# Turning x1 between two layers by DMA transposes instead of on TensorE

## The chip, the cores and the metric

The kernel runs on one core of one Trainium2 chip. The metric is the device time of one execution in microseconds, as the median of several runs. The engines of the core work side by side, each through its own list of instructions in order: TensorE (PE: products and transposes, into PSUM), VectorE (DVE), ScalarE (ACT), GpSimd (POOL) and SyncE (SP), which here issues every DMA transfer. An engine that waits for a semaphore holds up everything behind it in its list. A DMA issued on SyncE goes to the core's 16 DMA engines; SyncE is free again after the issue, and the data lands later.

## The reference

Two graph attention layers over 128 graphs of 64 nodes with 768 features, float32 throughout, each followed by a residual and a layer norm:

```python
# layer 0, 12 heads of 64 features
h = einsum('bnd,ade->bane', x, W)
th = tanh(h)
attn = leaky(th @ w_src + swap(th @ w_dst))           # slope 0.2
attn = softmax(where(adj, attn, -999.0))
feat = elu(heads_joined(attn @ h + b))
gate = sigmoid(x @ H_w.T + H_b)
x = layernorm(x + gate * feat + (1 - gate) * x)       # x1 below

# layer 1, 6 heads of 128 features
q, k, v = x @ Wq + bq, x @ Wk + bk, x @ Wv + bv       # split in heads
probs = softmax(q @ k.T / sqrt(128) + where(adj, 0, -9e15))
x = layernorm(x + x + heads_joined(probs @ v) @ Wf + bf)
```

## The kernel before

The 8192 rows (graphs times nodes) are cut into 64 tiles of 128 rows, two graphs to a tile. Two tiles form a pair, and there are 32 pairs (`NP`).

Every large product is a `Job`: a 256 x 768 by 768 x 768 product (one pair by one weight), done in seven block products instead of eight, by sums of blocks. For that, sums of the input's blocks (`block_sums`, s1 to s4) and sums of the weight's blocks are made on VectorE or POOL. A block product is three matmuls into a PSUM bank; `step` issues one product and then the way out (evictions to SBUF by ScalarE and VectorE) of the product before it.

Layer 0 is a loop of turns, one per pair `p`. The order of TensorE is written out by hand, in lists such as `TURN`. A letter names the job, a digit the product: h (features of layer 0), g (gate), v (the values of layer 1), all in lower case for the jobs of this turn; u is the value job begun in the turn before, H and G are the feature job of the next pair and the gate job of the pair before. `plan` hangs other work onto a position of the list: after the product at that position, the functions of the plan issue their instructions on all engines. A turn does, for the new pair `p` (tiles n0, n1): features, gate, the attention logits (`products`, `terms`, `logits`, `leaky`, `masked`, `exps`); and for the old pair `q = p - 1` (tiles t0, t1): turning the probabilities (`probs_by_nodes`, on TensorE), `attend`, `features`, `elu1`, `gated`, `stats` and `normed`, which yields x1, and then:

- `by_features` (L814) turns x1 of a tile, 128 rows by 768 features, into x1T, features by rows, which the value products and layer 1 need as an operand. Six 128 x 128 transposes on TensorE (L738) go into two PSUM banks, and two ScalarE copies (L739) bring them to SBUF.
- `value_sums` (L855) and the steps `v_sums` make the four block sums of x1T on VectorE, in the tiles sv.
- five of the seven value products v stand in the same turn (`TURN` L77), the last two (u4, u3) at the start of the next turn.
- `spill_features` (L826), `spill_values` (L851) and the store in `normed` (L810) write x1T, v and x1 to DRAM for layer 1.

The logits need one half of their terms spread over all partitions: `terms` (L665) stores 128 x 12 sums to DRAM (dstd) and reads them back broadcast (dd, two DMAs). `with_bias` (L682) issues two DMAs a tile that swap halves of h into hx, which `attend` needs.

SyncE issues all of these in program order, and a DMA waits at issue for what it reads or overwrites. A buffer that is used again is waited for by its next writer: the tag `work` rotates five buffers of 128 x 768, `x1T` and the four sv tiles have one buffer each.

After the last pair, a turn without new pair (`LAST`) runs the first query and key products of layer 1; then layer 1 runs over 16 groups of four tiles.

Of the kernel before, what the change touches and what calls it, by code (L numbers as in the profile page):

```python
# [10 lines left out]
U8 = mybir.dt.uint8  # L11
AF = mybir.ActivationFunctionType
# [3 lines left out]
P = 128  # L16
# [50 lines left out]
    "u4", "u3", "q1", "q2", "k1", "k2", "q6", "q5", "q7", "Q1", "q4", "Q2", "q3", "k6", "k5", "k7",  # L67
    "Q6", "k4", "k3", "v1", "v2", "v6", "v5", "v7", "K1", "v4", "v3",
]
LAST_REST = [(1, 2), (0, 5), (1, 6), (0, 7), (1, 5), (1, 7), (0, 4), (0, 3), (1, 4), (1, 3)]  # L70
LAST_AT = {3: 3, 4: 4, 5: 6, 6: 8, 7: 9, 8: 11, 9: 12, 11: 15, 12: 16, 15: 20, 16: 20, 19: 22}
# [6 lines left out]
    "h1", "h2", "u4", "u3", "h6", "g1", "h5", "h7", "g2", "g6", "h4",  # L78
    "h3", "g5", "g7", "v1", "v2", "g4", "v6", "g3", "v5", "v7",
]  # L80

THIRD_AT = {pos: max(pos - 2, 0) for pos in range(len(TURN))}
TURNS = {
    0: (FIRST, FIRST_AT, {}),
    1: (SECOND, SECOND_AT, SECOND_OLD),
    2: (TURN[2:], THIRD_AT, THIRD_AT),
}


@with_exitstack  # L90
def kernel(
# [40 lines left out]
    x1T_d = [dram.tile([P, KC, PAIR * P], F32, name=f"x1Td_{p}") for p in range(NP)]  # L132
    v_d = [dram.tile([P, D], F32, name=f"vd_{t}") for t in range(2 * NP)]
# [40 lines left out]
    def all_of(steps):  # L174
        for s in steps:
            s()

# [350 lines left out]
    with ExitStack() as ph, ExitStack() as ph_r:  # L528
# [21 lines left out]
        def sums_of(eng, pool, tag, t, name):  # L550
            return block_sums(
                eng,
                sum_tiles(pool, tag, P, name),
                t[:, :HK, :P],
                t[:, HK:, :P],
                t[:, :HK, P:],
                t[:, HK:, P:],
            )
# [17 lines left out]
        A[0], x_steps = sums_of(G, sbr, "sx", xTs[0], "x0")  # L576
# [78 lines left out]

        def products(t):

            h = st[t]["h"]
            th = sbr.tile([P, 2, D], F32, tag="th", name=f"th_{t}")
            S.activation(th[:, 1, :].rearrange("p (a e) -> p a e", e=E0), h[:, :, :E0], AF.Tanh)  # L660
            V.tensor_tensor(th[:, 0, :], th[:, 1, :], wsd[:, 0, :], ALU.mult)  # L661
            G.tensor_tensor(th[:, 1, :], th[:, 1, :], wsd[:, 1, :], ALU.mult)  # L662
            st[t]["th"] = th

        def terms(t):  # L665

            th = st[t].pop("th")
            sd = small.tile([P, 2 * H0], F32, tag="sd", name=f"sd_{t}")
            V.tensor_reduce(sd, th.rearrange("p s (a e) -> p (s a) e", e=E0), AX.X, ALU.add)
            st[t]["sd"] = sd  # L670
            nc.sync.dma_start(out=dst_d[t], in_=sd[:, :H0])
            dd = work(f"dd_{t}")
            for g in range(2):
                nc.sync.dma_start(
                    out=dd[g * N : (g + 1) * N, :],
                    in_=dst_d[t][g * N : (g + 1) * N, :]
                    .rearrange("m a -> (m a)")
                    .partition_broadcast(N),
                )
            st[t]["dd"] = dd  # L680
# [131 lines left out]
        x1Ts, B = {}, {}  # L812

        def by_features(t):  # L814
# [4 lines left out]
            for half in range(2):  # L819
                transposed(  # L820
                    x1Ts[p][:, 3 * half : 3 * half + 3, i * P : (i + 1) * P],
                    x1[:, half * HALF : (half + 1) * HALF],
                    f"x1Tp_{t}_{half}",
                )

# [29 lines left out]
        def value_sums(q):  # L855
            B[q], v_sums[q] = sums_of(V, sb, "sv", x1Ts[q], f"v{q}")

        def x_sums(p):
            operands, steps = sums_of(G, sbr, "sx", xTs[p], f"x{p}")
            all_of(steps)  # L860
            A.setdefault(p, {}).update(operands)

        def third_begins():
            x = xTs[2]
            A[2] = {1: x[:, :HK, :P], 2: x[:, HK:, :P]}
            jobs["H"] = h_job(2)
# [13 lines left out]
        for p in range(NP + 1):  # L880
# [3 lines left out]
            if new:  # L884
                jobs["G"] = jobs.get("g")
                jobs["h"], jobs["g"] = jobs["H"] if p == 2 else h_job(p), gate_job(p)
            plan = {}

            turn, of_new, of_old = TURNS.get(p, (TURN, {}, {})) if new else (LAST, {}, LAST_AT)
# [5 lines left out]
            def was(pos, *acts):  # L895
                at(pos, old, *acts, places=of_old)

# [3 lines left out]
            def v_begins():  # L901
                value_sums(q)
                jobs["v"] = v_job(q)


            was(0, do(probs_by_nodes, t1))
            at(0, old, do(exps, t0), do(gate_tanh, t1), places={0: 6} if p == 1 else of_old)
            was(1, do(residual, t1))
            was(2, do(attend, t1), do(gate_tanh, t0))
            was(3, do(features, t1), do(probs_by_nodes, t0), do(residual, t0))  # L910
            was(4, do(elu1, t1), do(gated, t1))
            was(5, do(attend, t0), do(stats, t1))
            was(6, do(features, t0), do(normed, t1))
            was(7, do(elu1, t0), do(gated, t0))
            was(8, do(by_features, t1), do(stats, t0))
            was(9, do(normed, t0))
            was(12, do(v_begins))
            was(15, lambda: v_sums[q][0](), lambda: v_sums[q][1](), do(spill_features, q))
            was(16, lambda: v_sums[q][2]())
            was(19, lambda: v_sums[q][3]())  # L920

            at(0, p + 1 < NP, do(load_xT, p + 1))
            at(3, new, lambda: adjs.__setitem__(p, load_adj(sb, 2 * p, PAIR, f"adj_{p}")))
            at(6, new, do(mask, p))
            at(4, 0 <= p - 2 < NP, do(spill_values, p - 2))
            at(8, new, do(inputs, p))
            at(11, new, do(products, n1))
            was(11, do(by_features, t0))
            at(12, new, do(products, n0))
            at(13, new, do(terms, n1), do(with_bias, n1))  # L930
            at(14, new, do(terms, n0), do(with_bias, n0))
            at(15, new, do(plus_one, p))
            at(16, new, do(logits, n1))
            at(17, new, do(leaky, n1))
            at(17, p + 1 < NP, do(x_sums, p + 1), places={17: 12} if p == 0 else of_new)
            at(18, new, do(masked, n1), do(logits, n0))
            at(19, new, do(exps, n1), do(leaky, n0))
            at(20, new, do(masked, n0))

            if p == NP - 1:  # L940
# [3 lines left out]
                for pos, block in ((2, B11), (3, B21), (8, T3), (15, B22)):  # L944
                    at(pos, True, do(load_block, wq, w0_w, block))
                for pos, block in ((6, B11), (9, B21), (19, T3), (19, B22)):
                    at(pos, True, do(load_block, wk, hw_w, block))
                at(16, True, q_sums[0])
                at(18, True, queries_begin, q_sums[1])
                at(19, True, lambda: all_of(row_sums[:2]))  # L950
            if p == NP:
                flush()
                for act in plan.pop(0):
                    act()
# [8 lines left out]
            if p == 1:  # L963
                at(14, True, third_begins, places={})
# [122 lines left out]
```

## Time and profile before

| | |
|---|---|
| median of 3 runs | 2967.19 us (2966.39 to 2970.22) |
| the profiled execution | 2970.77 us |
| its span | 2969.0 us |
| layer 0, one turn (45.62 us): TensorE transposes of x1 | 12, busy 1.64 us |
| the same turn: ScalarE copies of x1T | 4, busy 1.72 us |
| DMA over the span | 284.81 MB, mean 96 GB/s |

How the page is read: the span is the time from the first to the last instruction of one profiled execution. An engine's busy time is the sum of the time in which it worked; matmuls are pipelined, so lengths of neighbouring matmuls overlap, and the distance from start to start tells what one costs. The chain of waits goes back from the last instruction, at each step to what released it. A row of a group reads: line, engine, operation, output and input tiles, shape, count, busy time, mean length of one, idle time before, and who ended that idle time. A row of DMA issues reads: output and input, queue, count, size of one, and the median time from issue to landing. The granted clock is 1.00 in layer 0's turns.

### The profile page before, as it was taken

To read this page: it belongs to the slowest core of one execution; us is meant where nothing else is said; L and a number is where in the kernel's file an instruction comes from. 1 tells how busy PE (TensorE), PEld (TensorE's weight loads), DVE (VectorE), ACT (ScalarE), POOL (GpSimd) and SP (SyncE) were. 2 spreads that over 40 slices of the span, in tenths; PEclk is the share of its full clock that TensorE was granted. 3 is DMA by queue.
4 is the path that set the end of the run, shared out by engine and by line. 5 is a ranking of instruction groups with operands and counts; after the bars stand their busy time and mean duration, and the time that the engine had idled before them with its cause. 6 is when DMAs were issued, how large, how long until landed. Compare 5 with 4: busy or idle time off the path is not lost.

```text
span 2969.0 us, 45314 instructions
## 1 busy us (share of the span) xinstructions
PE 2925.2 (99%) x18048; PEld 2023.0 (68%) x18048; DVE 1796.9 (61%) x3017; ACT 1009.0 (34%) x1761; POOL 811.1 (27%) x650
## 2 busy tenths in 40 slices
PE   7999999999999999999999999999999999999999
PEld 4566666666666666666578777787777887777875
DVE  6878888788788878887844344333343443443345
ACT  2344344444443444444422222222222222222221
POOL 2434333333343333333422212211111212121121
PEclk9999999999999999999999999999999999999999
DMA  5333333334333333343532211222212222112221
GB/s 171 122 109 114 107 121 115 103 118 128 104 119 104 121 113 106 115 129 103 176 97 77 70 60 55 86 86 76 68 52 64 86 76 73 59 57 82 87 80 48
DMA packets 179681, 284.81 MB, mean 96 GB/s; under 512 B 46736, under 2 KB 113296, under 8 KB 179472
## 3 DMA queue, kind: packets, MB, share of 16 engines
q1 hardware_dynamic: 179472, 281.93, 29.1%
q8 instruction: 143, 2.34, 0.3%
q14 instruction: 66, 0.54, 0.1%
HBM read 167.81 MB, written 101.06 MB: 91 GB/s over the span
## 4 chain that ended last, share of the span: by engine, by line
PE 94%; DVE 3%; DMA 1%; ACT 1%; issue 0%; SPq 0%; POOLq 0%; POOL 0%; DVEq 0%; ACTq 0%
PE y_k L222 8%; PE y_o L222 8%; PE y_q L222 8%; PE y_v L222 8%; PE y_h L222 8%; PE y_g L222 8%; PE z_v L222 4%; PE z_o L222 4%; PE z_k L222 4%; PE z_h L222 4%; PE z_q L222 4%; PE z_g L222 4%; PE x_k L222 2%; PE x_o L222 2%; PE x_q L222 2%; PE x_h L222 2%
## 5 line engine op out<-in xcount | busy, mean ns | idle before, releaser
L789 POOL TENSOR_TENSOR x<-gate,x 128x768 f32<-128x768 f32 x64 | 117.4, 1835 | 323.8 <-ACT gate L840 309.0
L457 POOL TENSOR_TENSOR y<-y,bf_bc 128x768 f32<-128x768 f32 x64 | 115.3, 1832 | 311.4 <-DMA y<-x1d 311.4
L481 DVE TENSOR_TENSOR y<-y_o,y 128x384 f32<-128x384 f32 x128 | 71.4, 557 | 202.1 <-PE y_o L222 198.0
L339 DVE TENSOR_TENSOR kT<-z_k,kT 128x256 f32<-128x256 f32 x96 | 40.8, 425 | 239.3 <-PE z_k L222 136.1
L662 POOL TENSOR_TENSOR th<-th,wsd 128x768 f32<-128x768 f32 x64 | 117.2, 1832 | 182.5 <-DVE th L661 182.5
L274 POOL TENSOR_TENSOR rs_b<-ve_b,minus_half 128x1 f32<-128x1 f32 x64 | 35.1, 548 | 452.5 <-DVE ve_b L272 451.7
L192 POOL TENSOR_TENSOR sq_q<-a,a 128x768 f32<-128x768 f32 x16 | 29.2, 1828 | 432.8 <-PE y_o L222 286.9
L222 PE MATMUL y_h<-w_wq,xT 128*128 128x384 f32 x384 | 136.3, 492 | 8.6 <-DMA w_wq<-in_w_dram 7.9
L222 PE MATMUL y_k<-a,hw_wk 128*128 128x256 f32 x576 | 144.6, 387 | 0.0
L222 PE MATMUL y_q<-a,w_wq 128*128 128x256 f32 x576 | 140.9, 381 | 1.9 <-ACT qT L338 1.9
L222 PE MATMUL z_v<-wv,sv_v 128*128 128x384 f32 x384 | 138.9, 498 | 3.2 <-DVE v L652 3.2
L222 PE MATMUL y_q<-sq_q,w_wq 128*128 128x256 f32 x576 | 140.3, 380 | 0.9 <-ACT qT L338 0.9
L222 PE MATMUL y_h<-w_wq,sx_x 128*128 128x384 f32 x384 | 136.5, 492 | 4.2 <-ACT h L622 4.2
L222 PE MATMUL z_q<-sq_q,w_wq 128*128 128x256 f32 x576 | 140.1, 379 | 0.0
L222 PE MATMUL y_k<-sq_q,hw_wk 128*128 128x256 f32 x576 | 140.1, 379 | 0.0
L222 PE MATMUL z_k<-sq_q,hw_wk 128*128 128x256 f32 x576 | 140.0, 379 | 0.0
L338 ACT ACTIVATE qT<-y_q,bq_c 128x256 f32<-128x256 f32 x144 | 67.4, 469 | 213.2 <-PE y_q L222 213.2
L222 PE MATMUL y_v<-wv,sv_v 128*128 128x384 f32 x384 | 136.6, 492 | 3.0 <-DVE sv_v L193 3.0
L386 ACT ACTIVATE sc<-sc 128x512 f32<-128x512 f32 x48 | 30.2, 630 | 319.3 <-DVE sc L385 319.3
L222 PE MATMUL z_h<-w_wq,sx_x 128*128 128x384 f32 x384 | 137.6, 495 | 0.9 <-DVE w_wq L168 0.9
L222 PE MATMUL y_g<-hw_wk,sx_x 128*128 128x384 f32 x384 | 134.9, 488 | 2.4 <-DVE hw_wk L171 2.2
L222 PE MATMUL y_v<-wv,x1T 128*128 128x384 f32 x384 | 136.1, 491 | 1.2 <-ACT x1T L739 1.0
(171 smaller groups left out, 6678.1 us busy)
## 6 DMA issues: line engine op xcount, KB each, us to landing
x<-in_x_dram SPq DMA_DIRECT2D x64, 384.0 KB, 3.6
dd<-dstd SPq DMA_DIRECT2D x128, 192.0 KB, 3.4
x1d<-x SPq DMA_DIRECT2D x64, 384.0 KB, 2.6
x1Td<-x1T SPq DMA_DIRECT2D x32, 768.0 KB, 4.8
vd<-v SPq DMA_DIRECT2D x64, 384.0 KB, 2.9
a<-x1Td SPq DMA_DIRECT2D x64, 384.0 KB, 3.6
v<-vd SPq DMA_DIRECT2D x384, 64.0 KB, 2.3
y<-x1d SPq DMA_DIRECT2D x64, 384.0 KB, 4.1
```

The source lines that it names most:

```text
L192: lambda: e.tensor_tensor(s1, a21, a22, ALU.add),
L222: T.matmul(to[:, : self.n], lhsT, rhs, start=kc == 0 and not more, stop=kc == HK - 1, skip_group_check=more,)
L274: G.tensor_tensor(rstd, ve, minus_half, ALU.pow)
L338: lambda mn, bk_: S.activation(at(*mn), bk_, AF.Identity, bias=bias(mn[1])),
L339: lambda mn, bk_: V.tensor_tensor(at(*mn), bk_, at(*mn), ALU.add),
L386: S.activation(sc, sc, AF.Exp, scale=SCALE)
L457: G.tensor_tensor(y, y, pools["bf"], ALU.add)
L481: V.tensor_tensor(at(*mn), b, at(*mn), ALU.add)
L662: G.tensor_tensor(th[:, 1, :], th[:, 1, :], wsd[:, 1, :], ALU.mult)
L789: G.tensor_tensor(xp, st[t]["gate"], xp, ALU.mult)
```

## The change

For 28 pairs, 2 to 29, x1 is no longer transposed on TensorE. Float32 x1 is taken as words of 16 bits, and the low and the high halves are copied apart (`apart`), stored to DRAM (`send`), read back turned by six transposing DMAs (`turned`), each of 512 rows (low halves of 256 rows, then high halves) by 128 features, and joined to float32 again by four ScalarE copies (`joined`). The turned halves land in the tile sv, which later takes the four block sums as before. Pairs 0, 1, 30 and 31 still use `by_features`.

All seven value products of a pair now stand in the turn after the one that makes its x1; the first two products of the next pair's features (H1, H2) close a turn. The plan of the first two turns is kept in `of_opening`; all later ones follow `of_turn`. `products`, `terms` and `x_sums` are split so that their parts can stand at different positions.

```diff
 TURN = [
-    "h1", "h2", "u4", "u3", "h6", "g1", "h5", "h7", "g2", "g6", "h4",
-    "h3", "g5", "g7", "v1", "v2", "g4", "v6", "g3", "v5", "v7",
+    "h6", "h5", "g1", "u1", "h7", "u2", "g2", "u6", "h4", "u5", "h3", "u7",
+    "g6", "g5", "g7", "u3", "u4", "H1", "H2", "g4", "g3",
 ]
...
+    halves_d = [dram.tile([2, PAIR * P, D], U16, name=f"halvesd_{p}") for p in range(NP)]
...
+    def words(t):
+        return t.bitcast(U16).rearrange("p (e two) -> p two e", two=2)
...
+        def apart(t):
+            sp = work(f"sp_{t}").bitcast(U16).rearrange("p (two e) -> p two e", two=2)
+            x1 = words(st[t].pop("x1"))
+            if t % 2:
+                G.tensor_copy(sp[:, 0], x1[:, 0])
+            else:
+                S.copy(sp[:, 0], x1[:, 0])
+            S.copy(sp[:, 1], x1[:, 1])
+            st[t]["halves"] = sp
+
+        def send(t):
+            p, i = divmod(t, 2)
+            nc.sync.dma_start(
+                out=halves_d[p][:, i * P : (i + 1) * P, :].rearrange("h t d -> t h d"),
+                in_=st[t].pop("halves"),
+            )
+
+        def turned(p, *chunks):
+            if p not in sv:
+                sv[p] = sb.tile([P, 4, HK, P], F32, tag="sv", name=f"sv_{p}", bufs=1)
+            for c in chunks:
+                nc.sync.dma_start_transpose(
+                    out=landing(p)[:, c],
+                    in_=halves_d[p][:, :, c * P : (c + 1) * P].rearrange("h t f -> (h t) f"),
+                )
+
+        def landing(p):
+            return (
+                sv[p].rearrange("p s k t -> p (s k t)").bitcast(U16).rearrange("p (c ht) -> p c ht", c=KC)
+            )
+
+        def joined(p):
+            x1Ts[p] = sb.tile([P, KC, PAIR * P], F32, tag="x1T", name=f"x1T_{p}", bufs=1)
+            dst = x1Ts[p].bitcast(U16).rearrange("p c (t two) -> p two c t", two=2)
+            land = landing(p).rearrange("p c (two t) -> p two c t", two=2)
+            for kh in range(2):
+                for half in range(2):
+                    rows = slice(kh * HK, (kh + 1) * HK)
+                    S.copy(dst[:, half, rows], land[:, half, rows])
...
+            by_pe = old and q in (0, 1, NP - 2, NP - 1)
+            by_dma = old and not by_pe
...
+            def of_turn():
+                at(0, True, do(exps, t0))
+                at(0, p + 1 < NP, do(load_xT, p + 1))
+                at(1, True, do(probs_by_nodes, t1))
+                at(2, True, do(gate_tanh, t1), do(residual, t1))
+                at(3, True, do(attend, t1))
+                at(4, True, do(features, t1), do(probs_by_nodes, t0))
+                at(4, new, lambda: adjs.__setitem__(p, load_adj(sb, 2 * p, PAIR, f"adj_{p}")))
+                at(5, True, do(elu1, t1), do(gated, t1), do(gate_tanh, t0), do(residual, t0))
+                at(6, True, do(attend, t0), do(stats, t1))
+                at(7, True, do(features, t0), do(normed, t1))
+                at(7, new, do(mask, p))
+                at(8, True, do(elu1, t0), do(gated, t0))
+                at(8, by_dma, do(apart, t1))
...
+                at(9, True, do(stats, t0))
+                at(9, by_dma, do(send, t1))
+                at(9, new, do(tanh, n1), do(products, n1), do(inputs, p))
+                at(10, True, do(normed, t0))
+                at(11, by_dma, do(apart, t0))
+                at(12, by_dma, do(send, t0))
+                at(12, new, do(tanh, n0))
...
+                at(13, new, do(terms, n1), do(products, n0))
+                at(14, new, do(spread, n1))
+                at(15, new, do(terms, n0))
+                at(15, p + 1 < NP, do(next_begins, p + 1), do(x_sums, p + 1, 0))
+                at(16, new, do(spread, n0))
+                at(16, by_dma, do(turned, q, *range(KC)))
+                at(16, new, do(with_bias, n1), do(with_bias, n0), do(plus_one, p), do(logits, n1))
...
+                at(17, new, do(leaky, n1))
...
+                at(18, new, do(masked, n1), do(logits, n0))
+                at(18, True, do(spill_values, p - 2))
+                at(19, new, do(exps, n1))
...
+                at(20, new, do(leaky, n0), do(masked, n0))
+                at(20, by_dma, do(joined, q), do(v_begins))
+                at(20, p + 1 < NP, do(x_sums, p + 1, 1))
+                at(21, by_dma, v_sum(0), v_sum(1), do(spill_features, q), places={21: len(turn)})
+                at(22, by_dma, v_sum(2), places={22: len(turn) + 1})
+                at(23, by_dma, v_sum(3), places={23: len(turn) + 2})
```

A place of `len(turn)` or more is position 0, 1 or 2 of the next turn. `THIRD`, `NO_NEXT` and `LAST` are the lists of the third turn, of the last pair's turn and of the turn without a new pair; they are rewritten to the same pattern, `LAST` with 31 products for 27.

## The prediction

> **What bounds the kernel now.** I read the page's busy table and chain of waits first, then the busy time of one stretch, TensorE's and SyncE's timelines inside it, and last the rows that price a transfer.
>
> ```profile
> span 2969.0 us, 45314 instructions
> ...
> PE 2925.2 (99%) x18048; PEld 2023.0 (68%) x18048; DVE 1796.9 (61%) x3017; ACT 1009.0 (34%) x1761; POOL 811.1 (27%) x650
> ...
> PE 94%; DVE 3%; DMA 1%; ACT 1%; issue 0%; SPq 0%; POOLq 0%; POOL 0%; DVEq 0%; ACTq 0%
> ```
>
> TensorE is busy nearly all of the span and is 94% of the chain that ended last. Whatever leaves it is won, and whatever makes it wait is lost. Next, busy time by stretch. The columns are length, then busy time of PE, PEld, DVE, ACT and POOL, then granted clock, DMA share and GB/s.
>
> ```profile
> 701.68:747.30 45.62, 45.62 (x247) 27.69 (x246) 36.91 (x54) 20.02 (x32) 16.54 (x14) 1.00 0.35 114
> ...
> 1440.00:1530.00 90.00, 80.66 (x383) 54.77 (x380) 63.59 (x86) 29.93 (x52) 35.97 (x19) 0.94 0.36 123
> ```
>
> The first row is one turn of layer 0 (attention of one tile to the same point a pair later). TensorE has no idle time in it; VectorE has 8.7 us to spare, ScalarE 25.6, POOL 29. The waits that exist lie in the first 160 us and around the end of layer 0, the second row. So in the turns there is no wait to remove, and a gain can only come from work taken off TensorE. That work, in TensorE's timeline (start, length, engine, line):
>
> ```profile
> 716.12 0.82 PE L738 MATMUL x1Tp<-ident,x 128*128 128x128 f32 x6
> 716.77 2.10 PE L222 MATMUL y_g<-hw_wk,sx_x 128*128 128x384 f32 x6
> 718.71 2.10 PE L222 MATMUL y_h<-w_wq,xT 128*128 128x384 f32 x6
> ...
> 722.58 0.82 PE L738 MATMUL x1Tp<-ident,x 128*128 128x128 f32 x6
> 723.24 2.10 PE L222 MATMUL z_g<-hw_wk,sx_x 128*128 128x384 f32 x6
> ```
>
> Starts count, since lengths overlap. Six transposes of a tile hold TensorE for 716.77 - 716.12 = 0.65 us, the second tile's 0.66. One product (a step of the turn) takes 718.71 - 716.77 = 1.94 us.
>
> **What is removed.** 28 of the 32 pairs (2 to 29) are turned by DMA, the other four as before. TensorE loses 28 x (0.65 + 0.66) = 36.7 us. No product is added or dropped: seven per job, only the values' seven all stand one turn later. ScalarE loses four evictions of 0.482 us a pair.
>
> **What is added, and what covers it.** Per pair: three ScalarE copies and one POOL copy that part x1 into halves, two stores, six transposing DMAs on SyncE, and four ScalarE copies that join the halves. A ScalarE pass over 128x768 takes 0.84 us (the group of L849), so ScalarE gains 7 x 0.84 - 1.93 = 3.95 us and is at 24 of 44; POOL gains 1.0 to 1.8 us (its passes over 128x384 and 128x768). Both stay well below TensorE, so their volume costs nothing. VectorE's work is unchanged, but the four sums of x1T, 1.31 + 1.24 + 0.88 + 0.54 = 4.0 us, move to the start of the next turn. Their first reader there is u6 in step 8, the join's first reader is u1 in step 4.
>
> What decides is one date: when the last transpose has landed. I lay out one new turn, t = 0 at its first product, 45.62 - 1.31 = 44.3 us long. Step k ends at 1.94 k plus what is put in: 0.66 and 0.8 for the transposes of the probabilities after steps 2 and 5, 0.86 for each attention after steps 4 and 7.
>
> - The turn's logits come first on SyncE. Gate product g7 (step 15) ends at 32.4. The second tile's chain has by then run through ScalarE's tanh (31.3, after x1's norm at 28.3, its two halves and an eviction), VectorE's product (32.4), POOL's product of 1.83 (34.2) and VectorE's sum of 1.74: it ends at 36.0. That sum is stored and read back:
>
> ```profile
> 731.57 0.54 SPq L671 DMA_DIRECT2D dstd<-sd  x1
> 734.03 1.10 SPq L674 DMA_DIRECT2D dd<-dstd  x2
> ...
> 736.50 0.54 SPq L827 DMA_DIRECT2D x1Td<-x1T  x1
> 737.13 0.39 SPq L539 DMA_DIRECT2D xT<-in_xT_dram  x1
> 737.57 1.01 SPq L282 DMA_DIRECT2D adj<-in_adj_dram  x1
> ```
>
> - SyncE issues in order. From store to end of the second read-back issue it takes here 735.13 - 731.57 = 3.6 us (2.6 in the other tile of this turn), so the first transpose goes out at about 39.2. The two stores of the halves (issued by 30) and u3, the last reader of the tile it lands in (step 16, 34.4), are past by then.
> - The join waits for the landing on ScalarE, behind the second tile's leaky logits, which end at about 45.2 whatever the transposes do. Behind the join stand the exponentials of that tile, the eviction of h6 and the two evictions of the first tile's probabilities: 3.4 + 0.84 + 0.47 + 0.95 = 5.7 us. TensorE needs the last at the first attention, at 44.3 + 8.4 = 52.7. So the landing may be as late as 47.0, that is 7.8 us after the first issue; from there each us late is one us of TensorE per turn. At 9.1 (7.8 + 1.31) the gain is used up.
> - Queued on SyncE behind the transposes: four hx reads (first needed at that attention), two stores of values, the store of x1T, which waits for the join, and behind it the next xT (6.9 us to land, needed some 25 us later) and adj. The value store is waited for by u1's eviction on ScalarE; it has about 5 us to spare. They become late only after the join does.
>
> No transposing DMA is in the trace. The nearest rows:
>
> ```profile
> x<-in_x_dram SPq DMA_DIRECT2D x64, 384.0 KB, 3.6
> ...
> x1Td<-x1T SPq DMA_DIRECT2D x32, 768.0 KB, 4.8
> ...
> v<-vd SPq DMA_DIRECT2D x384, 64.0 KB, 2.3
> ...
> xT<-in_xT_dram SPq DMA_DIRECT2D x31, 768.0 KB, 6.9
> ```
>
> Six times 128 KB are the 768 KB of x1Td and xT, so the low bound is 4.8 us. By issues: five at 0.55 and the last landing in 2.3 (64 KB) to 3.6 (384 KB) gives 5.0 to 6.4. If each issue costs SyncE 1.01 as adj does, 5 x 1.01 + 3.6 = 8.7. The high bounds are six that do not overlap: 6 x 2.3 = 13.8 or 6 x 3.6 = 21.6. I take 6.4, as six issues back to back are nearest to dd's pair, which does overlap. That leaves 1.4 us to spare.
>
> The Trainium skill has two rules here that disagree, and no run shows either yet. "VectorE: DVE Perf Modes", section The three transpose paths, puts a 128x128 two-byte transpose at 1309 ns by DMA against 390 ns on TensorE and advises TensorE; the 24 such blocks of a pair, one after another, would be an estimated 31 us and would cost over 600 us in all. "DMA: Bandwidth & Descriptors", section Latency and other measured facts, gives 261 GB/s for DMA transposes of rows that are not contiguous, which is what is read here; 786 KB would then be an estimated 3.0 us and hide with my 6.4.
>
> Outside the turns: the last stretch has 9.3 us idle TensorE now, and the list of its last turn is rewritten (31 steps for 27). I add one more wait of the size of its 2.4 us row, with 5 us either way.
>
> **The sum.** The profiled execution took 2970.8 us, its span 2969.0 and 1.8 around it; it is 3.6 above the median of 2967.2, which the runs are measured by. From the profiled time: 2970.8 - 36.7 + 2.4 = 2936.5; from the median, 2932.9. I predict 2933 us for the median.
>
> **Rivals.**
>
> A, the landing is a little late: issues at 1.01, 8.7 us, 0.9 us of wait a turn: 2967.2 + 28 x (0.9 - 1.31) + 2.4 = 2958; at 9.1, no change. For it: SyncE has rows of 1.01 and of 0.55, and the read-backs of dd share the DMA engines at that moment. Against it: those engines are 35% busy over the turn.
>
> B, slower: the transposes do not overlap, and the join on ScalarE takes over as the bound. Place: ScalarE's wait for the last landing, then TensorE before the first attention. It decides from 9.1 us. At 13.8 us the wait is 6.0 a turn: 2967.2 + 28 x (6.0 - 1.31) + 2.4 = 3101. Idle time also costs clock:
>
> ```profile
> 1486.00:1488.50 2.50, 0.10 (x1) 0.02 (x1) 2.43 (x4) 0.00 (x0) 2.50 (x2) 1.00 0.00 1
> 1490.10:1493.50 3.40, 3.40 (x11) 2.72 (x10) 3.40 (x3) 1.15 (x3) 3.32 (x2) 0.58 0.02 5
> ```
>
> After 2.4 us of idle TensorE, 3.4 us ran at a granted 0.58; counted as half, that is up to 28 x 1.7 = 48 us more, 3149. For B: this is an operation no row shows, with sources in rows of 256 bytes, and only 1.4 us of cover. Against it: ordinary transfers from this queue do overlap (dd's two reads go out 0.55 apart and land 3.6 after issue).
>
> C, hidden anyway: would TensorE have waited in the place of the transposes? Its turns have no idle time and the engines slack, so this gives 2967, and I give it only the part of "same".
>
> **How the numbers follow.** Forecast (landing within 7.8 us) 0.45; A 0.17, of which 0.10 is still faster by over 0.2% (below 2961) and 0.07 within 0.2% of before, about what a measurement of this kernel can tell from no change; C 0.01; B and late cases beyond 9.4 us 0.37. So faster 0.55, same 0.08, slower 0.37. The forecast's own range is 2925 (36.7 won, 5 less waiting at the ends) to 2940. The range goes to 3060: a landing at 11 us, 3.2 us of wait a turn and most of the clock's loss (2967 + 53 + 40); of B, about half lies above it.
>
> **What would show it.** Right: no x1Tp group but for the four pairs, no wait of ScalarE at the join beyond 2 us, turns of 44.3 us without idle TensorE, first issue to last landing under 7.8 us. Wrong: probabilities' evictions named as what TensorE waits for, ScalarE waiting for a DMA into sv, SyncE's issues of the transposes at 1 us or more each, a granted clock below 1.00 inside the turns. A first transpose issued well before or after 39.2 would move the limit with it.

## The result, and the profile after

The changed kernel takes 3079.38 us (median of 4, 3075.88 to 3086.19) against 2968.68 us of the kernel before beside it: 1.0376 times, 95% interval [1.0364, 1.0389]. It is slower by 111 us where 34 us less were forecast, and 19 us above the range. The profiled execution has this page (span, busy time, chain of waits):

```profile
span 3076.6 us, 45130 instructions
...
PE 2943.9 (96%) x17712; PEld 2016.0 (66%) x17712; DVE 1780.3 (58%) x3017; ACT 1124.8 (37%) x1845; POOL 884.0 (29%) x678
...
PE 70%; DVE 16%; ACT 5%; issue 4%; DMA 2%; POOL 1%; SPq 1%; DVEq 0%; POOLq 0%; ACTq 0%
```

TensorE has 336 instructions fewer, as meant, and yet is busy 19 us longer. Its share of the chain fell from 94% to 70%, and VectorE's rose from 3% to 16%. So TensorE both waits and runs more slowly. What it waits for in the turns (stretch 160 to 1440 us; total, times, longest):

```profile
PE y_g L239 <- DVE gate L655: 73.4, 26, 2.8
PE av L786 <- ACT pT L766: 0.5, 1, 0.5
```

This is one wait of 2.8 us in every turn, for VectorE's eviction of a gate product (26 turns lie in the stretch). The probabilities (pT), which the prediction watched, appear once, with 0.5 us. Three timelines of one turn show where that eviction was held up (start, length, engine, line). TensorE:

```profile
755.67 2.10 PE L239 MATMUL y_v<-wv,sv 128*128 128x384 f32 x6
757.61 2.10 PE L239 MATMUL y_g<-hw_wk,sx_x 128*128 128x384 f32 x6
759.54 2.10 PE L239 MATMUL z_g<-hw_wk,sx_x 128*128 128x384 f32 x6
764.47 3.90 PE L239 MATMUL y_g<-hw_wk,sx_x 128*128 128x384 f32 x6 [2.83 <-DVE gate L655]
```

ScalarE and then VectorE, of the same kernel:

```profile
760.36 1.03 ACT L295 ACTIVATE x<-x,sh_a,rs_a 128x768 f32<-128x768 f32 x1 [3.39 <-DVE sh_a L294]
761.42 0.83 ACT L860 COPY sp<-x 128x768 uint16<-128x768 uint16 x1
762.16 0.83 ACT L861 COPY sp<-x 128x768 uint16<-128x768 uint16 x1
762.89 0.47 ACT L668 COPY v<-y_v 128x384 f32<-128x384 f32 x1
```

```profile
763.39 0.56 DVE L669 TENSOR_TENSOR v<-z_v,v 128x384 f32<-128x384 f32 x1 [2.60 <-ACT v L668]
763.87 0.55 DVE L655 TENSOR_TENSOR gate<-y_g,hb_bc 128x384 f32<-128x384 f32 x1
764.33 1.74 DVE L689 TENSOR_REDUCE sd<-th 128x24 f32<-128x1536 f32 x1
```

Read it backwards. The second y_g is gate product g7. It needs the bank in which g6 (757.61) stands, so it waits for VectorE's addition of g6 (L655, 763.87). On VectorE that addition is queued behind the addition of the value product u7 (L669), which needs ScalarE's copy of u7 (L668). TensorE finished u7 at 757.77, but ScalarE ran that copy only at 762.89, because it stands in program order behind x1's norm of the pair's first tile (L295) and the two copies of its halves (L860, L861). ScalarE itself sat idle for 3.39 us waiting for that norm's input. So a product that was ready at 757.77 was evicted 5.1 us late by an idle engine, and two more engines queued behind it. In the kernel before, the norms ran at 713.49 and 719.30 of the turn shown there and its next eviction of values only at 729.24: no value product stood near a norm.

The same turn by busy time, then the wait and what follows it (length; busy PE, PEld, DVE, ACT, POOL; granted clock; DMA share; GB/s):

```profile
730.95:779.82 48.87, 46.04 (x236) 27.24 (x235) 35.46 (x54) 23.34 (x35) 18.88 (x15) 0.97 0.45 138
761.64:764.47 2.83, 0.00 (x0) 0.00 (x0) 1.07 (x3) 2.83 (x5) 0.21 (x1) 1.00 0.54 209
764.47:767.90 3.43, 3.43 (x6) 1.97 (x7) 2.47 (x2) 1.10 (x2) 0.88 (x1) 0.54 0.18 59
```

After the 2.83 us without work TensorE gets 0.54 of its clock for 3.43 us: g7 takes 768.21 - 764.47 = 3.74 us from start to start instead of 1.94, another 1.80 us. Between the first and the 26th of these turns (the halves' first copy, 175.77 and 1397.70) lie 25 turns, 48.88 us each in the mean, from 47.16 to 50.20. The wait is 2.8 us in all of them; what differs is the clock behind it, here after the waits that end at 185.35, 232.51 and 714.29:

```profile
185.35:188.80 3.45, 3.45 (x11) 2.12 (x12) 3.42 (x4) 1.10 (x2) 0.90 (x1) 1.00 0.18 59
232.51:235.90 3.39, 3.39 (x6) 1.96 (x7) 2.47 (x2) 1.10 (x2) 0.84 (x1) 0.53 0.18 60
714.29:719.50 5.21, 5.21 (x8) 2.86 (x9) 3.40 (x4) 1.10 (x2) 2.66 (x2) 0.50 0.25 86
```

So the 1.80 us of the turn shown is near the mean of a loss that runs from 0.1 to 3.1 us. Without wait and loss a turn comes to 48.87 - 2.83 - 1.80 = 44.24 us, and the turn from 185.35 to 232.51, which has hardly any loss, gives the same: 47.16 - 2.82 - 0.10. The forecast was 44.3. The turns lose 28 x (48.88 - 45.62) = 91 us. The rest, 16 us by the two profiled executions and 20 by the medians, lies outside them; it is what is left over, not a sum of waits. TensorE's wait for the gate in the third turn (3.8 us, none before) belongs to it, and these waits from 1440 to 1640 us:

```profile
PE y_q L239 <- DMA a<-x1Td: 12.2, 1, 12.2
PE y_g L239 <- DVE gate L655: 5.6, 2, 2.8
PE x1Tp L765 <- ACT x L295: 3.8, 1, 3.8
```

The two waits of y_g here are the last two of the 28 turns; the other two lie at the end of layer 0, where the longest wait in the kernel before was 3.2 us. Last, the transposes: SyncE's timeline, the issues' own figures (ns, least, median and most; then us to landing), and ScalarE's join that waits for them.

```profile
722.83 1.08 SPq L701 DMA_DIRECT2D dd<-dstd  x2
724.02 8.08 SPq L876 DMA_TRANSPOSE sv<-halvesd  x6
```

```profile
L876 SPq DMA_TRANSPOSE sv<-halvesd x168: 1144/1258/2433, 194.2 to 1522.6; - x168
...
DMA to landing us min/median/max: 2.6/2.8/4.6
```

```profile
730.23 1.98 ACT L893 COPY x1T<-sv 128x768 uint16<-128x768 uint16 x2 [0.19 <-DMA sv<-halvesd]
733.68 1.98 ACT L893 COPY x1T<-sv 128x768 uint16<-128x768 uint16 x2 [1.47 <-DMA sv<-halvesd]
```

The last one landed 733.68 - 724.02 = 9.66 us after the first went out. That is later than the 7.8 us that the prediction allowed, and yet TensorE does not wait for it here.

### The profile page after: what moved, and what is told of

It is laid out like the page before. It is cut to its first block, busy times and chain, and to the rows that moved or that the text cites. A ratio compares the mean times of both kernels' runs of the same rounds, so it can differ in the third digit from the quotient of the medians.

```text
span 3076.6 us, 45130 instructions
## 1 busy us (share of the span) xinstructions
PE 2943.9 (96%) x17712; PEld 2016.0 (66%) x17712; DVE 1780.3 (58%) x3017; ACT 1124.8 (37%) x1845; POOL 884.0 (29%) x678
## 4 chain that ended last, share of the span: by engine, by line
PE 70%; DVE 16%; ACT 5%; issue 4%; DMA 2%; POOL 1%; SPq 1%; DVEq 0%; POOLq 0%; ACTq 0%
PE y_o L239 8%; PE y_k L239 8%; PE y_q L239 8%; PE y_g L239 7%; PE y_v L239 4%; PE z_o L239 4%; PE y_h L239 4%; PE z_k L239 4%; PE z_q L239 4%; DVE ex L826 3%; PE z_v L239 2%; DVE fo L803 2%; PE x_o L239 2%; PE x_k L239 2%; DVE st_a L285 2%
## 5 line engine op out<-in xcount | busy, mean ns | idle before, releaser
L239 PE MATMUL y_g<-hw_wk,sx_x 128*128 128x384 f32 x384 | 178.4, 613 | 81.5 <-DVE gate L655 79.0
L816 POOL TENSOR_TENSOR x<-gate,x 128x768 f32<-128x768 f32 x64 | 136.6, 2135 | 373.8 <-ACT gate L909 373.8
L239 PEld LDWEIGHTS y_g<-hw_wk,sx_x 128*128 128x128 f32 x384 | 86.3, 233 | 157.4 <-DVE gate L655 96.3
L683 POOL TENSOR_TENSOR th<-th,wsd 128x768 f32<-128x768 f32 x64 | 116.8, 1824 | 181.6 <-DVE th L682 181.6
L810 ACT ACTIVATE ex<-fo,minus_one 128x768 f32<-128x768 f32 x64 | 59.9, 935 | 276.5 <-DVE fo L803 276.5
L239 PE MATMUL y_q<-a,w_wq 128*128 128x256 f32 x576 | 143.6, 387 | 12.2 <-DMA a<-x1Td 12.2
L239 PE MATMUL z_v<-wv,sv 128*128 128x384 f32 x384 | 144.6, 516 | 0.0
L712 POOL TENSOR_TENSOR h<-h,b_bc 128x768 f32<-128x768 f32 x64 | 140.3, 2214 | 0.0
```

Of the source, the lines that this page charges most:

```text
L239: T.matmul(to[:, : self.n], lhsT, rhs, start=kc == 0 and not more, stop=kc == HK - 1, skip_group_check=more,)
L712: G.tensor_tensor(h[:, :, :E0], h[:, :, :E0], b01_bc.unsqueeze(1).to_broadcast([P, H0, E0]), ALU.add)
L810: S.activation(ex, fo, AF.Exp, bias=minus_one)
L816: G.tensor_tensor(xp, st[t]["gate"], xp, ALU.mult)
```

## The experiments

Times are medians; ratios are against the kernel before in the same series, with 95% intervals. In the diffs `do`, `at(pos, ...)` and the jobs are those of the plan shown above.

**One: is it the order?** The first tile's norm and halves go two positions later, behind u7.

```diff
-                at(10, True, do(normed, t0))
-                at(11, by_dma, do(apart, t0))
-                at(12, by_dma, do(send, t0))
+                at(12 if by_dma else 10, True, do(normed, t0))
+                at(12, by_dma, do(apart, t0))
+                at(13, by_dma, do(send, t0))
```

> The norm of the second tile and the copies of its halves are issued one position later, so that on ScalarE the eviction of u7 stands ahead of them. Theory 'order' (g7 waits for VectorE's eviction of g6, which stands behind the sum of u7, which waits for ScalarE's eviction of u7, which stands behind the norm and 1.6 us of halves): the 2.8 us wait of y_g for gate L655 goes, with it the clock's dip, and a turn falls from 49.6 to between 44.3 and 46.5 us; 2935 to 2995 us, the upper part if the landing (9.5 us after the first issue) then becomes the wait at the first attention. Theory 'landing' (the join waiting for the transposes is what lengthens the turn): the wait stays, 3060 to 3090 us.

Measured 2986.56 us, 1.0063 [1.0048, 1.0078]: 93 us of the 111 are back with no work changed. The wait for the gate's eviction is gone from the turns, the clock over the turns is 1.00, a turn takes 45.71 us in the mean. What TensorE waits for now, and ScalarE's timeline ahead of one such wait:

```profile
PE av L786 <- ACT pT L766: 30.8, 28, 2.4
```

```profile
747.05 0.84 ACT L735 ACTIVATE att<-att 128x768 f32<-128x768 f32 x1 [1.27 <-DVE att L725]
747.80 1.96 ACT L893 COPY x1T<-sv 128x768 uint16<-128x768 uint16 x2
750.67 1.96 ACT L893 COPY x1T<-sv 128x768 uint16<-128x768 uint16 x2 [0.91 <-DMA sv<-halvesd]
752.50 0.83 ACT L754 ACTIVATE prob<-att 128x768 f32<-128x768 f32 x1
753.23 0.47 ACT L639 COPY h<-y_h 128x384 f32<-128x384 f32 x1
753.59 0.87 ACT L766 COPY pT<-pTp 128x384 f32<-128x384 f32 x2
```

This is the wait that the prediction had foreseen: the join on ScalarE, with 0.91 us of waiting for the landing in it, then the exponentials and an eviction, and only then pT. It costs 1.1 us a turn, and it was hidden in the changed kernel because g7's wait and the slow clock after it move the first attention 4.6 us later in the mean.

**Two: or the volume on ScalarE?** Both half copies of the first tile go to POOL instead, where one of the second tile's runs already; the order stays (`S.copy(sp[:, i], x1[:, i])` becomes `G.tensor_copy(...)`).

> Both copies of the second tile's halves, and one of the first tile's as before, run on POOL. Theory 'order': the eviction of u7 stands behind the norm alone, so y_g waits 1.6 us less, about 1.2 us; if the clock does not dip for so short a wait, a turn loses 1.2 us instead of 4.6: 2985 us; with the dip 3030. Theory 'landing': no change, 3070 to 3090.

Measured 2994.20 us, 1.0086 [1.0071, 1.0101]; a wait of 1.2 us a turn for the gate's eviction stays (33.9 us in the turns), without a slow clock behind it. Taking the copies out of the queue helps nearly as much as putting them elsewhere in it, and leaves the part that is ScalarE's idle wait for the norm itself.

**Three: or the landing?** This kernel leaves out three of the six transposes of each pair; the join reads the first three twice.

```diff
-                at(16, by_dma, do(turned, q, *range(KC)))
+                at(16, by_dma, do(turned, q, *range(HK)))
```

> Leaves out three of the six transposes of a pair; the join fills both halves of x1T from the three that are made, so x1T, the values and layer 1's queries and keys are not the reference's. Theory 'order': the landing is 3.8 us or more earlier and the waits of y_g for gate L655 stay at 2.8 us in each turn: 3065 to 3085 us. Theory 'landing': the lengthening of the turn goes with it, 2935 to 2985 us.

Measured 3079.24 us, 1.0379 [1.0363, 1.0394]: not a microsecond, and the wait for the gate's eviction is the same 73.4 us. ScalarE's idle time for the landing fell from 32.9 us in all to 1.9, so the landing did come earlier. In the changed kernel the transposes' landing decides nothing.

**Four: the price of an issue.** As one, with twelve transposes of 256 rows instead of six of 512.

> As e1, with twelve transposes of 256 rows for the six of 512. If the issue costs by rows, each takes 0.6 to 0.7 us and the time is that of e1, 2975 to 2995 us; if it costs by instruction, each takes about 1.26 us, the last landing is 7.5 us later, and the wait at the first attention grows by about as much: 3180 to 3250 us with the clock's dips.

A single execution took 3231.48 us; an issue still took 1.24 us in the median, against 1.26. So the price is one of the instruction, not of its rows. TensorE's waits for pT reach 7.6 us each, 197 us in all: once the landing is late enough, the wait that the prediction watched does bound the turn.

**Five to eight: attempts on the join.** Each starts from the first experiment. Here the join's second half is put behind the first tile's evictions, and the sums of the values two steps later:

> As e1, and the second half of the join stands behind the first tile's probabilities on ScalarE, with the sums of x1T two positions later. If after e1 the landing of the last three transposes is what the first attention waits for, this takes 1 to 3 us a turn off e1: 2930 to 2950 us. If e1 has no such wait, the same as e1 within 0.3%.

Measured 3088.71 us, 1.0405 [1.0388, 1.0422], a miss. TensorE's wait only changes its place; then a sum on VectorE beside a product on POOL:

```profile
PE pTp L765 <- DVE rden L802: 93.2, 29, 3.8
```

```profile
750.46 2.16 DVE L212 TENSOR_TENSOR sv<-x1T,sv 128x384 f32<-128x384 f32 x1
```

```profile
750.08 2.12 POOL L816 TENSOR_TENSOR x<-gate,x 128x768 f32<-128x768 f32 x1 [8.73 <-DVE gate L655]
```

The sums now stand ahead of the normalised attention (rden, fo) on VectorE, and the last of them runs at the same time as POOL's product and takes 2.16 us instead of 0.55. With the sums right behind that attention instead:

> As e4 (e1 with the join in two parts), but VectorE's four sums of x1T stand behind the features of the first tile. Theory for e4's loss (features t1 stood behind sums that waited for the second half of the join, and TensorE needs the banks that these features free): the 3.3 us wait of pTp for rden goes, and the wait for pT with it: 2950 to 2975 us. If e4's loss has another cause, 3050 us or more.

Measured 3001.92 us, 1.0110 [1.0096, 1.0123]; two small waits stand in the turns (pT 16.1 us, the values' evictions 11.0). Sending three of the transposes a step earlier, ahead of the second read-back of the logits:

> As e1, with the transposes of chunks 0 to 2 issued one position earlier, right behind u3 and ahead of the second tile's store and read-back of the logits' sums. Theory 'order, then landing' (after e1 what is left in the turns is the wait of the first attention for pT on ScalarE, 1.1 us a turn, because ScalarE stands in the join until the sixth transpose has landed; each costs SyncE 1.26 to 1.4 us): the landing comes 3 to 4 us earlier, those 30.8 us of waits go to under 5, and the time is 2950 to 2962 us. If instead the logits, now read back later, are what the turn waits for, 2985 to 3010 us.

Measured 2997.85 us, 1.0099 [1.0085, 1.0113]. The join no longer waits for a DMA, but SyncE issues in order, so the second tile's read-back is later by the three issues, its leaky logits with it, and these hold up ScalarE as long: pT still 32.3 us in all. The same with the last list changed (u6 and u5 ahead of q1, two weight loads behind the reads of x1T):

> As e5, with the end of layer 0 changed: u6 and u5 ahead of q1, and the loads of x1T for the first queries issued ahead of the last two weight blocks of Wk. Of the 12.4 us in which q1 waits for those loads, 4 are covered by the two products and 1 to 3 come from the earlier issue: 5 to 8 us less than e5, 2942 to 2957 us, at or a little below the kernel before (2968).

Measured 2998.16 us, 1.0093 [1.0079, 1.0107], no gain: the 11.2 us of y_q went, and y_v waits 7.3 us for ScalarE and y_q 4.7 us instead.

**Nine and ten: the join off ScalarE,** wholly, then by half (`S.copy` in `joined` becomes `G.tensor_copy`, and POOL's last two sums of x go ahead of it).

> The first tile's x1 is normed behind gate product g6's eviction, as in e1_evict_first; besides, all four copies that join the halves run on POOL, behind its last two sums of x, and none on ScalarE. In e1 a turn without its wait would be 45.71 - 30.1/27 = 44.6 us, and POOL has nothing between 745.7 and 756.2 of the window whose join begins at 747.8. Theory (what e1 still loses is ScalarE's time in front of the first attention's probabilities): the wait of av for pT falls below 5 us in the profile, the turn goes to 44.5 to 44.9 us, and the time is e1's 2986.6 less 20 to 33: 2954 to 2967, at or below the kernel before. Rival one (the landing is what is late: join's second half waits for the last transpose until 750.7, and the values' sums and u1 then wait wherever the copies run): TensorE waits for v's evictions or for sv (y_v, z_v) instead, over 20 us, and the time stays at 2980 to 2990. Rival two (POOL's copies share a port with VectorE and slow its sums and leaky logits): VectorE's tensor_tensor of 0.55 us become 1.5 to 2.2 us beside the copies, POOL's copies exceed 1.5 us, and features of the second tile come late: pTp waits for rden or fo, 2990 to 3060.

> As e9_join_on_pool, but the first two copies of the join (features 0 to 383, already landed) stay on ScalarE and only the last two, which wait for the last transposes, run on POOL. Theory (ScalarE is held by the wait for the landing and the copies behind it, about 2.9 us of its 4.9, rather than by all four): the wait of av for pT falls from 30 us to below 8, the turn to 44.6 to 45.0, the time to 2957 to 2970. If the volume on ScalarE counts and not the wait alone, half of the 30 us stays and e9 is 10 to 15 us faster than this one. If POOL's copies beside VectorE are the trouble, this one is faster than e9.

Measured 2995.35 us, 1.0089 [1.0076, 1.0101], and 2986.72 us, 1.0061 [1.0047, 1.0075]: misses both, with 25.8 and 28.1 us of waiting for pT. The first one's ScalarE tells why:

```profile
749.52 0.84 ACT L735 ACTIVATE att<-att 128x768 f32<-128x768 f32 x1 [1.27 <-DVE att L725]
753.54 0.84 ACT L754 ACTIVATE prob<-att 128x768 f32<-128x768 f32 x1 [3.18 <-DVE att L748]
754.29 0.46 ACT L639 COPY h<-y_h 128x384 f32<-128x384 f32 x1
754.65 0.86 ACT L766 COPY pT<-pTp 128x384 f32<-128x384 f32 x2
```

With the join gone ScalarE is idle for 3.18 us, waiting for VectorE's masked logits of the first tile; and the evictions of the second tile's probabilities, which need nothing of that, stand behind those exponentials. It is the mistake of the change once more: ready work behind a waiting instruction.

**Eleven and twelve: the exponentials behind those evictions.** First on the tenth kernel, then on the first experiment, with the whole join on ScalarE again.

```diff
-                at(0, True, do(exps, t0))
                 at(0, p + 1 < NP, do(load_xT, p + 1))
-                at(1, True, do(probs_by_nodes, t1))
+                at(1, True, do(probs_by_nodes, t1), do(exps, t0))
```

> As e10_join_shared, and the exponentials of the first tile (ScalarE, 0.84 us) stand behind the two evictions of the second tile's probabilities instead of ahead of them. Theory (in e10 the av for pT wait of 27.1 us over 27 turns is no longer the join's but the order on ScalarE: its exponentials start 753.18 after VectorE's late logits of the other tile end, and pT, whose own data are long ready, stands behind them and one eviction): with the exponentials out of the way pT is evicted at once, the wait in the turns falls below 3 us and the time is 2986.7 less 24 to 28: 2958 to 2964, below the kernel before. Rival one (the wait returns at the next station, the first tile's probabilities: pTp waits for ScalarE's prob, or the second attention for its pT): a new wait of 0.5 to 1 us a turn, time 2975 to 2987. Rival two (the turn is bounded elsewhere, by VectorE's logits chain): the turn stays at 45.5 us with no single wait named.

> As e1_evict_first, with the whole join on ScalarE, and the exponentials moved behind the second tile's probabilities as in e11_shared_exps_after. If what e1 loses is the 4.9 us that the join with its wait for the landing takes on ScalarE, pT still stands behind the join's end (752.5 in e1's window) and one eviction, and gains only the exponentials' 0.75 us: the wait falls from 30 us by 27 x 0.75 = 20 us to about 10, the time to 2966 to 2970, that is no better than before and 5 to 12 us above e11. If the join's place does not matter and only the exponentials' does, this kernel and e11 agree within 3 us.

On the tenth: 3007.09 us, 1.0135 [1.0119, 1.0150], a miss; the copies on POOL are now the late ones, POOL's product of the gate meets the sums again (L211 at 2.17 us), and features of the second tile come late (rden, 30.8 us). On the first: 2971.14 us, 1.0008 [0.9999, 1.0017]. ScalarE now works through this stretch with one gap of 0.44 us, and the waits for pT fell to 12.8 us:

```profile
743.19 1.96 ACT L893 COPY x1T<-sv 128x768 uint16<-128x768 uint16 x2
745.59 1.96 ACT L893 COPY x1T<-sv 128x768 uint16<-128x768 uint16 x2 [0.44 <-DMA sv<-halvesd]
747.42 0.47 ACT L639 COPY h<-y_h 128x384 f32<-128x384 f32 x1
747.78 0.86 ACT L766 COPY pT<-pTp 128x384 f32<-128x384 f32 x2
748.52 0.86 ACT L754 ACTIVATE prob<-att 128x768 f32<-128x768 f32 x1
```

Two changes of order and no change of work have taken back 108 of the 111 us. The gain that was forecast is not there, though. A turn takes (1398.77 - 177.71) / 27 = 45.22 us in the mean, 0.40 less than before and 1.0 more than 44.24. Of that 1.0 us, 0.47 are the waits for pT, and an attention that waited takes 0.28 us longer to the next product (794.54 - 793.40 = 1.14 instead of 0.86); the rest is not accounted for. And of the 28 x 0.40 = 11 us won in the turns nothing arrives: by the medians 14 us are lost outside them.

**Thirteen and fourteen: outside the turns.** In the third turn the values' sums are emitted four steps later; the thirteenth also changes the end of layer 0.

```diff
-                at(16, by_pe, v_sum(0), v_sum(1), do(spill_features, q))
+                at(16 if p != 2 else 20, by_pe, v_sum(0), v_sum(1), do(spill_features, q))
...
-                at(17, by_pe, v_sum(2))
+                at(17 if p != 2 else 20, by_pe, v_sum(2))
```

> As e12_exps_after, with the two places outside the regular turns changed. At the end of layer 0: the last turn's list begins u1 u2 u6 u5 q1 instead of u1 u2 q1, the second tile's leaky logits and the exponentials of the first are emitted behind u2 and u5 so that the evictions of u1 and u2 stand ahead of them on ScalarE, and two blocks of wk are loaded behind the four reads of x1T. In the third turn the values' sums are emitted four steps later, behind gate product g7's eviction. Theory (of e12's 20 us of TensorE idle outside the regular turns that the kernel before does not have, 10.5 are products that wait for reads which SyncE issues at the same date as before, 1469.1 against 1467.9, so that only ready products ahead of them help, and 3.9 are VectorE's sums ahead of an eviction): the wait of y_q for a falls from 10.5 to below 5 us, the wait of y_g for gate from 3.9 to below 1, nothing of that size comes in their place, and the time is 2971.1 less 8 to 14: 2957 to 2963, below the kernel before. Rival (the end is bounded by the last pair's own chain from the logits to the attention, and not by what TensorE has ready): as in e7_three_before_end the wait moves to y_v for ScalarE's eviction or to pTp, av for pT, and the time stays within 4 us of 2971.

> As e12_exps_after, with the third turn's sums of the values alone moved behind gate product g7's eviction; the end of layer 0 is e12's again. In e13_ends the first regular turn began 8.8 us earlier than in e12 (168.95 against 177.71), but the whole gained only 5.9: so the third turn was worth 8 to 9 us (3.9 of waiting, the rest clock and the waits near it) and the new list at the end cost about 3. Theory: this kernel takes 2971.1 - 8.8 = 2962.3 us (2960 to 2965), ahead of the kernel before and of e13. Rival (the end is bounded by the last pair's own chain, and absorbs what comes earlier ahead of it): the wait of y_q for a grows by what is gained, from 10.5 to 14 us or more, and the time is 2966 to 2971.

Measured 2965.25 us, 0.9985 [0.9976, 0.9994], and 2964.14 us, 0.9984 [0.9975, 0.9993]: the only two below the kernel before, by 3 to 5 us, which is less than 0.2%. In the fourteenth the first regular turn begins 177.71 - 169.74 = 8.0 us earlier than in the twelfth, and 7.0 us of it arrive in the time. What is left in it from 1395 to 1660 us begins with:

```profile
PE y_q L239 <- DMA a<-x1Td: 12.0, 1, 12.0
PE x1Tp L765 <- ACT x L295: 3.8, 1, 3.8
```

The wait of y_q grew from 10.5 us in the twelfth to 12.0. Layer 1's reads wait on SyncE behind two blocks of weights and a store of values. They go out at 1467.91 in the kernel before, and in the twelfth and the fourteenth:

```profile
1469.12 2.87 SPq L325 DMA_DIRECT2D a<-x1Td  x4
```

```profile
1459.17 3.25 SPq L325 DMA_DIRECT2D a<-x1Td  x4
```

The twelfth's date is nearly that of the kernel before, but it is no fixed date: with turns that come earlier the reads went out 9.95 us earlier, and only 1.5 us more were spent waiting for them. The thirteenth, with more ready products ahead, traded this wait for 10.9 us of waiting for ScalarE's evictions and was no better. What would shorten the end, the date of these reads or that of the last pair's logits, is not settled.

## Why the prediction was wrong, point by point

- **What bounds the kernel, and what is won.** Right: TensorE bounds the turns, and what is left of a turn of the changed kernel without the new wait and its loss of clock is 44.24 us (forecast 44.3). The 1.31 us a turn were taken off TensorE and given back in the same turn. No kernel here ran such a turn: the best means are 45.22 and 45.14 us, in the twelfth and the fourteenth.
- **"Both stay well below TensorE, so their volume costs nothing. ... What decides is one date: when the last transpose has landed."** This is the step that failed. An engine at half load that issues in order has no free place for a copy behind an instruction that waits. The hand-laid turn even had "an eviction" in ScalarE's queue behind the norm and its two halves, and followed it to the tanh and the logits, but not to VectorE's addition, g6's bank and g7. Both the norm (laid to end at 28.3, it ended at 761.39 - 730.95 = 30.4) and the three instructions behind it belong to that date; g7 started at 764.47 - 730.95 = 33.5 instead of 30.4. Moving the values' products into the next turn is what brought an eviction there. Experiments one and three show both halves of this: the order is worth 93 us, the landing nothing.
- **The landing.** The first issue was placed well: it went out 724.02 - 680.77 = 43.2 us after that turn's first product, or 37.3 without the 5.9 us that TensorE lost in that turn (2.83 of waiting, 2.06 in g7, 1.05 in u3). The forecast was 39.2, between the 38.6 and 39.6 that its two rows for store and read-back give. The landing was mis-sized: 9.66 us against 6.4 taken and 4.8 to 21.6 bounded, because an issue costs 1.26 us and not 0.55. One copy of the join took 1.05 us, not 0.84. The limit of 7.8 us was passed, and the wait it announced came out once the first was gone: 1.1 us a turn in experiment one, where the prediction's own formula with 9.66 us gives 1.9.
- **Of the skill's two rules,** the Trainium skill's "VectorE: DVE Perf Modes", The three transpose paths, led to an estimated 31 us block by block and its "DMA: Bandwidth & Descriptors", Latency and other measured facts, to an estimated 3.0 us by bandwidth; the trace's 9.66 us agrees with neither, since the time goes by issues.
- **Rival B** had the right sign and nearly the size (3101 and up to 3149), by the wrong door: transposes do overlap, and it named pT and the join as the place. So its nearness is luck. Its price of the clock held in the mean: 1.7 us after each wait forecast, 1.8 measured, though single turns lost 0.1 to 3.1. Experiment four shows the wait that B named, but again with transposes that overlap.
- **Outside the turns** 2.4 us were forecast with 5 either way; it was 16 to 20. The prediction counted waits of the old trace there and gave the rewritten lists one more of 2.4 us; what came was a wait of 3.8 us in the third turn and one of 12.2 us for layer 1's reads (1.9 before). The third turn's share is about 7 us, as experiment fourteen shows against twelve; the cause of the rest stays open. (`LAST` has 32 products, not the 31 counted.)
- **The sum that holds:** 2967 + 28 x (2.83 + 1.80 - 1.38) + 19 = 3077 us, where 1.38 is 45.62 - 44.24 and the 19 us outside the turns are what was left over, so they are fitted and not priced.

## What to carry to other kernels

Busy shares do not price an instruction on an engine that issues in order: for each instruction put into a queue, list the ready evictions that then stand behind it and follow each one through to the bank it frees. When a change moves products to another place, look for instructions that wait (a norm, a landing, a read-back) ahead of the places where their evictions now fall, and put the evictions first. And check the places outside the loop by themselves: the twelfth kernel's turns are 11 us shorter in all than those of the kernel before, and it is no faster.

## What the runs showed of the hardware

- A transposing DMA cost SyncE about as much an issue with 512 rows as with 256: 1.26 and 1.24 us in the median (others here: 0.33 for the store of x1, 0.54 to 0.6 for dd and hx, 1.25 for adj). They overlap in flight: each landed 2.8 us after its issue, six in 9.66 us.
- The length of a wait alone did not decide whether TensorE's granted clock fell. In the changed kernel the wait of 2.8 us cost no clock in 6 of the 28 turns (1.00 after 185.35); in the others it fell, to 0.53 over 3.4 us after 232.51 and 0.50 over 5.2 us after 714.29. A wait of 1.58 us in the twelfth was followed by 0.69 over 5.5 us (at 1335.86), waits of 1.76 and 2.42 us in the first by 1.00 (at 754.22 and 1347.50). None of the 1.2 us waits for the gate in the second cost any. What decides is not shown.
- VectorE's additions of two SBUF tiles took longer beside a product on POOL: 0.55 us became 2.16 (128x384, experiment four), and the last step of the residual (L828, 128x768) took up to 2.39 us and 1.63 in the mean in the changed kernel, against 0.96 before, where POOL's work fell elsewhere. An eviction from PSUM did not: L640 at 760.24 of the changed kernel took 0.55 us inside a product of POOL (L683, 760.05 to 761.86).
